# Four quantizer levels ahead of VectorE, and a transposed router product, in a fused weight-quantize and FFN kernel

## The chip, the cores and the metric

The kernel runs on one core of a Trainium2 chip. A core has five engines with a queue of instructions each: TensorE (PE; its weight loads are shown apart as PEld), VectorE (DVE), ScalarE (ACT), GpSimd (POOL) and SyncE (SP, which only issues DMAs here). The metric is the device time of one execution in microseconds; lower is better. Before the change it is 2672.33 us, the median of 3 runs (2671.02 to 2674.37).

## The reference

All is float32. Cut to what matters:

```python
# conditioner: a quantized linear layer with a low-rank part
lora_delta = lora_B @ lora_A * 0.5
cb = codebook / max(|codebook|)                    # 32 values
wg = (weight + lora_delta).reshape(O, I // 128, 128)
normalized = wg / exp(scale_log)
thresholds = (cb[:-1] + cb[1:]) * 0.5              # 31
idx = searchsorted(thresholds, normalized, side='left')
w = (cb[idx] - normalized) + normalized            # straight-through
w_eff = (w * scale).reshape(O, I) + lora_delta
c = x @ w_eff.T
# FFN: base product plus a mixture of 8 rank-16 experts
result = c @ W_base.T + b_base
ax, probs = c @ A_w.T, softmax(c @ router_w.T)
mixed = einsum(einsum(ax, cores), probs)
return x + result + (mixed @ B_w.T) * 2.0
```

x has 4096 rows of 2048, all weights are 2048 x 2048. The thresholds need not be sorted, so the kernel sorts them first and finds for each interval the value that the reference's search gives.

## The kernel before

The product x @ w_eff.T @ W_base.T is taken as x times one folded matrix. So there are two stages.

**Weight stage.** The quantized weight is made in 16 strips of 128 input columns (index i; a strip's tiles are w and a, 128 x 2048 each, in two halves f of 8 blocks). Each finished strip is multiplied with W_base into one strip of the folded matrix, and with the 24 columns of A_w and router_w (ra_sb) for the router.

A strip goes through these steps. In the strip before, its preparation: `delta` (TensorE, the low-rank part of w), `scaled` (ScalarE, half of a gets that part times a constant), `normalize` (GpSimd, w plus that, divided by the scale), `level_0` (ScalarE, Relu then Sign into sg, then Identity into a: the initial contents, the lowest value or the one after the first threshold) and `more_levels` (GpSimd, for levels 1 and 2: a compare-and-multiply into lv, line 526, and an addition to a, line 527). Then its own turn, `quantize`: for each level r from 3 to 30, `raise_to` lets ScalarE make a mask (line 537, Relu with a huge gain into float8, four buffers) and VectorE copies the level's value into a where the mask is set (line 538). Then `straight_through` (GpSimd, lines 557 to 559: minus w, plus w, times scale, half after half). Strip 0 has 29 full levels and two in halves, and its preparation is on VectorE.

The order of all other work is written out by hand. In strip i's turn, `behind(step, f, ...)` puts an operation behind the level of that step (step = r-3), in program order; each engine and each DMA queue then runs its own part of that order and waits for data or for a free buffer. In strip i's turn fall:
- at its start, the last quarter of products (3,1) of strip i-2, `route(i-2)`, `delta(i+1, 0)`;
- `products(i-1, ...)`: with blocks b of W_base, 0 and 1 kept on chip (wb), 2 and 3 streamed in quarters (wbp, three buffers, each `load_piece` on SP right after the quarter that it follows); blocks (2,0) first, then (3,1); `low_rank` ends each;
- `multiply_router(i-1)`: 16 matmuls with the strip as weights and 24 columns of ra_sb moving, and one for the low-rank part;
- `keep` (ScalarE copies a block from PSUM, a DMA writes it to wc_dram) and `keep_router` (copies 24 columns into rac);
- `load_w`, `load_la`, `load_route` (four tiles xs of xT) on SP. `route` is eight matmuls of 512 columns on a quarter of the array's columns each (line 642), adding the router's part for all tokens into acc. PSUM has three buffers m for products and router;
- from strip 5 to 15, `made`: one block of the folded matrix of four earlier strips (two blocks in strip 15) is fetched from wc_dram into up, transformed on GpSimd (`outer_w`, `inner_pair`, for a product that saves multiplications) and put into s_dram by SP. The fetch is at step 0, the rest at the steps of `step_of`.

After strip 15 come its own products, the last transforms (late_columns, and last_fetch with what follows it), with VectorE doing its straight-through in quarters.

**Main stage.** TensorE runs 196 products (line 909) of the transformed x (xA, xB, xC from xT, t on VectorE) with the tiles s of s_dram, two levels of a scheme with 7 products in place of 8; the other engines combine the results. Its code is not changed.

These few lines carry the preparation and the order before:

```python
for c in (1, 3):
    v.tensor_scalar(lv, half(i, f, "w"), base[:, c + 1 : c + 2], base[:, c : c + 1], ALU.is_gt, ALU.mult)
    v.tensor_tensor(a, a, lv, ALU.add)
```

Of the kernel before, what the change touches and what calls it, by code (L numbers as in the profile page):

```python
# [21 lines left out]
P = 128  # L22
# [4 lines left out]
MIX_SCALE = 32.0 / 16.0  # L27


def quantizer_tables(nc, work, const, psum, cb, index, beside):  # L30
# [109 lines left out]
    base = const.tile([P, 5], F32, name="base")  # L140
    v.tensor_tensor(base[:, 0:1], step[:, 0:1], cb[:, 0:1], ALU.subtract)
    next(beside, None)
    v.tensor_copy(base[:, 2:3], step[:, 0:1])
    next(beside, None)
    v.tensor_tensor(base[:, 1:2], step[:, 1:2], base[:, 2:3], ALU.subtract)
    next(beside, None)
    v.tensor_copy(base[:, 3:4], step[:, 1:2])
    next(beside, None)
    v.tensor_tensor(base[:, 3:4], step[:, 2:3], base[:, 3:4], ALU.subtract)
    next(beside, None)  # L150
    v.tensor_scalar(base[:, 2:5:2], neg_t[:, 1:3], -1.0 / GAIN, None, ALU.mult)
    next(beside, None)
    return neg_t, step, base
# [34 lines left out]
def adaln_ffn_kernel(  # L188
# [72 lines left out]
    nc.gpsimd.memset(rac, 0.0)  # L261
    cb = const.tile([P, K], F32, name="cb")
    ident = const.tile([P, P], F32, name="ident")
    ones = const.tile([P, 1], F32, name="ones")

# [7 lines left out]
    def constants():  # L273
        make_identity(nc, ident)
        nc.gpsimd.memset(cores_sb, 0.0)

        nc.gpsimd.tensor_copy(ones, ident[:, Q : Q + 1])
        for j in range(1, 4):
            nc.gpsimd.tensor_tensor(ones, ones, ident[:, RP * j + Q : RP * j + Q + 1], ALU.add)
        for j in range(4):  # L280
            nc.sync.dma_start(cores_sb[:, j, 0:Q], cores)
            for rows, what in ((slice(RP * j, RP * j + Q), bwT), (slice(RP * j + Q, RP * j + Q + 1), bias)):
                nc.sync.dma_start(
                    bw_sb[rows].rearrange("q (f n) p -> q f n p", n=2),
                    what.rearrange("q (f j n p) -> q j f n p", j=4, n=2, p=P)[:, j],
                )
# [80 lines left out]
    with ExitStack() as sa:  # L367
# [4 lines left out]
        xsp = sa.enter_context(tc.tile_pool(name="xsp", bufs=4))  # L372
# [61 lines left out]
        with tc.tile_pool(name="tables", bufs=1) as tables:  # L434
# [20 lines left out]
            neg_t, step, base = quantizer_tables(nc, tables, const, psum_t, cb, index, first_scales)  # L455
# [23 lines left out]
        ra_sb = cl.tile([P, NM, NRA], F32, name="ra_sb")  # L479
        nc.sync.dma_start(ra_sb, raT)  # L480
# [29 lines left out]
        def level_0(i, f, part):  # L510
            q, a = half(i, f, "w"), half(i, f, "a")
            if part == 0:
                strips[i]["sg"] = mpool0.tile([P, NM // 2, P], BF16, tag="sg", name=f"sg_{i}_{f}")
                nc.scalar.activation(strips[i]["sg"], q, AF.Relu, bias=neg_t[:, 0:1], scale=GAIN)  # L514
            sg = strips[i]["sg"]
            if part == 1:
                nc.scalar.activation(sg, sg, AF.Sign)
            if part == 2:
                nc.scalar.activation(a, sg, AF.Identity, bias=cb[:, 0:1], scale=base[:, 0:1])  # L519

        def more_levels(i, f):
            a = half(i, f, "a")
            lv = mpool0.tile([P, NM // 2, P], F32, tag="lv", name=f"lv_{i}_{f}")
            v = nc.gpsimd
            for c in (1, 3):
                v.tensor_scalar(lv, half(i, f, "w"), base[:, c + 1 : c + 2], base[:, c : c + 1], ALU.is_gt, ALU.mult)  # L526
                v.tensor_tensor(a, a, lv, ALU.add)  # L527

# [13 lines left out]
        def quantize(i, at):  # L542

            for r in range(3 if i else 2, T):
                raise_to(i, r, new_mask(i, r), 0, 1)
                for do in at.get(r - 3, []):
                    do()

# [14 lines left out]
        lora_r = cl.tile([R, NRA], F32, name="lora_r")  # L563
# [19 lines left out]
        def lora_router():  # L583
            ps = psum_m.tile([P, OQ], F32, tag="m", name="lc_r")
            for m in range(NM):
                nc.tensor.matmul(
                    ps[:R, :NRA], lora_B_sb[:, m, :], ra_sb[:, m, :], start=(m == 0), stop=(m == NM - 1)
                )
            nc.scalar.mul(lora_r, ps[:R, :NRA], LORA_SCALE)
# [24 lines left out]
        def multiply_router(i):  # L614
            ps = psum_m.tile([P, OQ], F32, tag="m", name=f"m_{i}_r")
            for m in range(NM):
                nc.tensor.matmul(
                    ps[:, :NRA], strips[i]["a"][:, m, :], ra_sb[:, m, :], start=(m == 0), stop=False
                )
            nc.tensor.matmul(ps[:, :NRA], strips[i]["la"][:R], lora_r, start=False, stop=True)  # L620
            strips[i]["r"] = ps

# [5 lines left out]
        def keep_router(i):  # L628
            nc.scalar.copy(rac[:, strip[i], 0:NRA], strips[i]["r"][:, :NRA])


        def load_route(i):
            strips[i]["x"] = []
            for n in range(4):
                x = xsp.tile([P, 2 * HT], F32, tag="xs", name=f"xs_{i}_{n}")
                nc.sync.dma_start(x, xT[ts(strip[i], P), ts(n, 2 * HT)])
                strips[i]["x"].append(x)

        def route(i):
            for n in range(8):  # L640
                j = n % 4
                nc.tensor.matmul(
                    acc[n // 4][RP * j : RP * j + RP],
                    rac[:, strip[i], :],
                    strips[i]["x"][n // 2][:, ts(n % 2, HT)],
# [77 lines left out]
        for i in range(NS):  # L723
# [5 lines left out]
            if i > 1:  # L729

                products(i - 2, (3, 1), NC - 1)
                route(i - 2)
                behind(5, keep, i - 2, 3)
                behind(6, keep, i - 2, 1)
            if i + 1 < NS:
                delta(i + 1, 0)
                if i > 0:
                    behind(3, load_w, i + 1)
                behind(7, scaled, i + 1, 0)
                behind(8, normalize, i + 1, 0)  # L740
                for f, (a, b, c) in enumerate(((10, 12, 14), (16, 18, 20))):
                    behind(a, level_0, i + 1, f, 0)
                    behind(b, level_0, i + 1, f, 1)
                    behind(c, level_0, i + 1, f, 2)
                    behind(c, more_levels, i + 1, f)
                behind(11, scaled, i + 1, 1)
                behind(11, normalize, i + 1, 1)
            if i > 0:


                behind(9, load_route, i - 1)
                for c in range(2):
                    behind(2 + 3 * c, products, i - 1, (2, 0), c)
                if i + 1 < NS:
                    behind(7, delta, i + 1, 1)
                for c in range(2, NC):
                    behind(2 + 3 * c, products, i - 1, (2, 0), c)
                behind(13, multiply_router, i - 1)
                behind(17, keep, i - 1, 2)
                behind(19, keep, i - 1, 0)  # L760
                for c in range(NC - 1):
                    behind((17, 20, 22)[c], products, i - 1, (3, 1), c)
                behind(22, keep_router, i - 1)
                if i + 2 < NS:
                    behind(20, load_la, i + 2)
            else:
                behind(4, nc.vector.reciprocal, rflat[:, NM:], flat[:, NM:])
# [3 lines left out]
                behind(26, lora_router)  # L771
            for n, (g, b) in enumerate(made.get(i, [])):
                step_of = (4, 9, 11, 12, 15, 26, 27) if len(made[i]) == 1 else (
                    (4, 6, 8, 9, 10, 12, 13) if n == 0 else (17, 19, 21, 22, 23, 25, 26)
# [30 lines left out]
        route(last - 1)  # L805
        keep(last - 1, 3)
        keep(last - 1, 1)
        load_route(last)
# [4 lines left out]
        for bs in ((2, 0), (3, 1)):  # L813
            for c in range(NC):
                products(last, bs, c)
            if bs[0] == 2:
                multiply_router(last)
            for b in bs:
                keep(last, b)
            if bs[0] == 2:  # L820
                keep_router(last)
                late_columns()
        route(last)
# [412 lines left out]
```

## Time and profile before

| | |
|---|---|
| median of 3 runs | 2672.33 us |
| the profiled execution, its own time | 2673.15 us |
| its span, first to last instruction | 2671.4 us |
| weight stage, first to last predicated copy | 19.2 to 1179.4 us |
| main stage's first product (line 909) | 1247.1 us |
| PE busy, share of the span | 2550.7 us, 95% |
| DVE busy | 1574.0 us, 59% |
| ACT busy | 1107.3 us, 41% |
| POOL busy | 1302.6 us, 49% |
| TensorE's mean granted clock | 0.973 |

In the profile's lines, an entry reads: line of the code, engine, operation, output <- inputs, shape, count. "Idle before" is how long the engine did nothing just ahead of it, and what ended that. A share over the whole span hides that there are two stages: VectorE is busy to the brim in the first and little used in the second. Stretches of the timeline tell more, and the start of line 557 marks the end of each strip.

### The profile page before, as it was taken

The numbers are of one execution on the slowest core, as the hardware profiler recorded it, in microseconds if no ns is written. First come the engines' busy times: TensorE is split into PE (matmuls) and PEld (weight loads), VectorE is DVE, ScalarE is ACT, GpSimd is POOL, SyncE is SP. The second block draws the span as 40 slices with busy tenths as digits, with TensorE's granted clock in tenths as the row PEclk, the third lists the DMA queues.
The fourth block names the chain that finished last, engine by engine and source line by source line (L and its number), as shares of the span: only waits on it lengthen the run. The fifth ranks groups of instructions, "written<-read, shape, count | busy, mean of one in ns | idle before, by whom it ended". The sixth has DMA issues, their size and how long they took to land.

```text
span 2671.4 us, 26221 instructions
## 1 busy us (share of the span) xinstructions
PE 2550.7 (95%) x10544; PEld 1758.3 (66%) x10544; DVE 1574.0 (59%) x996; ACT 1107.3 (41%) x740; POOL 1302.6 (49%) x755
## 2 busy tenths in 40 slices
PE   5599999999999999999999999999999999999999
PEld 2244444444444444446888888888888888888887
DVE  9999999999999999973433222242133322214221
ACT  7889988889888888940000000000000000000000
POOL 5566668889888888844413140042320323202224
PEclk9799999999999999999999999999999999999999
DMA  8254457767777766699844666545675455754554
GB/s 317 108 173 174 176 178 251 240 222 233 247 240 237 243 229 230 211 313 350 325 173 163 225 249 217 197 146 204 241 236 194 166 205 174 277 211 174 193 199 159
DMA packets 222041, 581.06 MB, mean 218 GB/s; under 512 B 18328, under 2 KB 119584, under 8 KB 176992
## 3 DMA queue, kind: packets, MB, share of 16 engines
q1 hardware_dynamic: 215360, 557.96, 60.7%
q0 software_dynamic: 4960, 14.95, 1.6%
q10 hardware_dynamic: 1600, 6.49, 0.6%
q8 instruction: 83, 1.36, 0.2%
q14 instruction: 38, 0.31, 0.0%
HBM read 477.62 MB, written 101.71 MB: 217 GB/s over the span
## 4 chain that ended last, share of the span: by engine, by line
PE 53%; DVE 25%; ACT 7%; POOL 6%; DMA 6%; issue 2%; SPq 0%; DVEq 0%; POOLq 0%; ACTq 0%
PE z L909 49%; DVE a L538 24%; ACT above L537 5%; DMA w<-in_weight 2%; PE m L606 2%; POOL a L558 1%; POOL a L557 1%; PE z L939 1%; DMA xA<-in_xT 1%; POOL w L505 1%; POOL a L559 1%; POOL w L430 1%; DMA wc_dram<-out 1%; ACT sg L514 1%; DMA s_dram<-late 1%
## 5 line engine op out<-in xcount | busy, mean ns | idle before, releaser
L538 DVE COPY_PREDICATED a<-above,step 128x2048 f32<-128x2048 uint8 (+1 forms) x453 | 1112.9, 2460 | 45.8 <-ACT above L537 1.5
L537 ACT ACTIVATE above<-w,neg_t 128x2048 fp8e5<-128x2048 f32 (+1 forms) x453 | 888.9, 1991 | 80.1 <-DVE a L538 67.1
L909 PE MATMUL z<-t,s 128*128 128x256 f32 x3584 | 793.0, 381 | 4.6 <-DVE u L991 4.6
L909 PEld LDWEIGHTS z<-t,s 128*128 128x128 f32 x3584 | 678.7, 190 | 108.5 <-issue 12.9
L606 PE MATMUL m<-wbp,a 128*128 128x512 f32 x1024 | 505.3, 640 | 74.8 <-POOL a L559 60.3
L606 PE MATMUL m<-wb,a 128*128 128x512 f32 x1024 | 460.7, 592 | 0.2
L606 PEld LDWEIGHTS m<-wbp,a 128*128 128x128 f32 x1024 | 205.3, 205 | 326.4 <-issue 243.0
L606 PEld LDWEIGHTS m<-wb,a 128*128 128x128 f32 x1024 | 193.7, 190 | 242.3 <-issue 237.2
L989 ACT COPY m<-z 128x1024 f32<-128x1024 f32 x28 | 28.4, 1013 | 763.3 <-PE z L909 763.3
L1000 POOL TENSOR_TENSOR c<-u,m 128x1024 f32<-128x1024 f32 x16 | 50.1, 3130 | 444.1 <-DVE u L997 422.8
L909 PE MATMUL z<-xA,s 128*128 128x256 f32 x1152 | 254.6, 379 | 0.0
L909 PEld LDWEIGHTS z<-xA,s 128*128 128x128 f32 x1152 | 218.8, 190 | 30.5 <-issue 0.8
L526 POOL TENSOR_SCALAR lv<-w,base 128x1024 f32<-128x1024 f32 x60 | 226.9, 3782 | 3.6
L1000 POOL TENSOR_TENSOR M<-u,m 128x1024 f32<-128x1024 f32 x8 | 24.8, 3103 | 330.2 <-DVE u L997 288.2
L909 PE MATMUL z<-xB,s 128*128 128x256 f32 x768 | 169.7, 379 | 0.0
L909 PE MATMUL z<-xC,s 128*128 128x256 f32 x768 | 169.7, 379 | 0.0
L991 DVE TENSOR_TENSOR u<-z,m 128x1024 f32<-128x1024 f32 x28 | 34.3, 1223 | 216.1 <-issue 172.6
L909 PEld LDWEIGHTS z<-xB,s 128*128 128x128 f32 x768 | 145.9, 190 | 19.8
L909 PEld LDWEIGHTS z<-xC,s 128*128 128x128 f32 x768 | 145.9, 190 | 19.8
L995 ACT COPY m<-z 128x1024 f32<-128x1024 f32 x28 | 28.3, 1011 | 308.5 <-PE z L909 308.5
L527 POOL TENSOR_TENSOR a<-a,lv 128x1024 f32<-128x1024 f32 x60 | 142.4, 2374 | 16.9 <-ACT a L519 12.3
L557 POOL TENSOR_TENSOR a<-a,w 128x1024 f32<-128x1024 f32 x30 | 71.3, 2378 | 145.0 <-DVE a L538 145.0
(208 smaller groups left out, 1922.8 us busy)
## 6 DMA issues: line engine op xcount, KB each, us to landing
s<-s_dram SPq DMA_DIRECT2D x196, 1024.0 KB, 4.8
wbp<-in_wbT SPq DMA_DIRECT2D x131, 1024.0 KB, 5.2
xs<-in_xT SPq DMA_DIRECT2D x64, 512.0 KB, 7.3
xA<-in_xT SPq DMA_DIRECT2D x24, 1024.0 KB, 9.1
s_dram<-z SPq DMA_DIRECT2D x84, 256.0 KB, 5.7
xB<-in_xT SPq DMA_DIRECT2D x16, 1024.0 KB, 10.8
outT<-M SPq DMA_DIRECT2D x16, 1024.0 KB, 10.6
w<-in_weight SPq DMA_DIRECT2D x15, 1024.0 KB, 7.7
```

The costliest lines, as they stand in the source:

```text
L430: v.tensor_tensor(w, w, r.unsqueeze(2).to_broadcast([P, NM // 2, P]), ALU.mult)
L526: v.tensor_scalar(lv, half(i, f, "w"), base[:, c + 1 : c + 2], base[:, c : c + 1], ALU.is_gt, ALU.mult)
L527: v.tensor_tensor(a, a, lv, ALU.add)
L537: nc.scalar.activation(above[:, c], q, AF.Relu, bias=neg_t[:, r : r + 1], scale=GAIN, saturate=False)
L538: nc.vector.copy_predicated(a, above[:, c].bitcast(U8), step[:, r : r + 1].to_broadcast([P, F // n]))
L557: v.tensor_tensor(a, a, w, ALU.subtract)
L606: nc.tensor.matmul(ps, strips[i]["a"][:, CM * c + m, :], t[:, m, :], start=c == 0 and m == 0, stop=False)
L909: nc.tensor.matmul(z[:, c, :], s[:, k, ts(c, P)], rhs[:, k, :], start=not more and k == 0 and c % PER == 0, stop=k == NK - 1 and c % PER = ...
L989: nc.scalar.copy(temp("m1", o), z["a"])
L991: nc.vector.tensor_tensor(temp("u2", o), z["b"], state["m1", o], ALU.add)
L995: nc.scalar.copy(temp("m5", o), z["c"])
L1000: lambda d: nc.gpsimd.tensor_tensor(d, state["u3", o], state["m5", o], ALU.add),
```

## The change

The constant NL = 4 is the number of levels that are in a before VectorE begins. Strips 1 to 15 now start `quantize` at r = 4, so step k is level k+4. Level 3 of half 0 is made by ScalarE (Relu, Sign, then a copy with a scale into a tile lx) and added to a by GpSimd (`last_level`). Level 3 of half 1 is made by GpSimd as levels 1 and 2 are, except for strips 6 to 15 (those prepared while GpSimd also has a transform; `half_step`), where VectorE still raises that half by a copy of 128 x 1024.

The router's product is transposed: the 32 columns of ra_sb (24 and zeros) are the weights, the strip moves, and the 16 matmuls go to four quarters of the array's columns in turn. `router_parts` (ScalarE) copies the four partial sums to raw, and `router_sum` (TensorE) adds and transposes them by a product with stack, four identities one above the other. `keep_router` now copies all 32 columns.

`route` and `load_route` are split into halves with two xs buffers in place of four; the second half is loaded at step 0 of the next strip and used at step 8. `load_w` comes at step 1 in two halves. Most steps of ScalarE's and GpSimd's work are new: the preparation of half 0 ends later, and `keep` of blocks 2 and 0 comes at steps 16 and 17.

```diff
+NL = 4
...
+    v.tensor_copy(rise[:, 1:NL], step[:, 0 : NL - 1])
+    v.tensor_tensor(rise[:, 0:1], step[:, 0:1], cb[:, 0:1], ALU.subtract)
+    v.tensor_tensor(rise[:, 1:NL], step[:, 1:NL], rise[:, 1:NL], ALU.subtract)
+    v.tensor_scalar(past, neg_t[:, 0:NL], -1.0 / GAIN, None, ALU.mult)
...
-    nc.gpsimd.memset(rac, 0.0)
...
+        nc.gpsimd.tensor_copy(stack, ident[:, 0:RP])
...
+            nc.gpsimd.tensor_tensor(stack, stack, ident[:, RP * j : RP * j + RP], ALU.add)
...
-        xsp = sa.enter_context(tc.tile_pool(name="xsp", bufs=4))
+        xsp = sa.enter_context(tc.tile_pool(name="xsp", bufs=2))
...
-        ra_sb = cl.tile([P, NM, NRA], F32, name="ra_sb")
-        nc.sync.dma_start(ra_sb, raT)
+        ra_sb = cl.tile([P, NM, RP], F32, name="ra_sb")
+        nc.vector.memset(ra_sb, 0.0)
+        nc.sync.dma_start(ra_sb[:, :, 0:NRA], raT)
...
-        def level_0(i, f, part):
+        def scalar_level(i, f, r, part):
...
-            if part == 2:
-                nc.scalar.activation(a, sg, AF.Identity, bias=cb[:, 0:1], scale=base[:, 0:1])
+            if part == 2 and r == 0:
+                nc.scalar.activation(a, sg, AF.Identity, bias=cb[:, 0:1], scale=rise[:, 0:1])
+            elif part == 2:
+                strips[i]["lx"] = mpool0.tile([P, NM // 2, P], F32, tag="lx", name=f"lx_{i}_{f}")
+                nc.scalar.activation(strips[i]["lx"], sg, AF.Copy, scale=rise[:, r : r + 1])
+
+        def half_step(i):
+            return i - 1 in made
...
-            for c in (1, 3):
-                v.tensor_scalar(lv, half(i, f, "w"), base[:, c + 1 : c + 2], base[:, c : c + 1], ALU.is_gt, ALU.mult)
+            for r in range(1, NL - 1 if f == 0 or half_step(i) else NL):
+                v.tensor_scalar(lv, half(i, f, "w"), past[:, r : r + 1], rise[:, r : r + 1], ALU.is_gt, ALU.mult)
                 v.tensor_tensor(a, a, lv, ALU.add)
+
+        def last_level(i, f):
+            a = half(i, f, "a")
+            nc.gpsimd.tensor_tensor(a, a, strips[i]["lx"], ALU.add)
...
-            for r in range(3 if i else 2, T):
+            if half_step(i):
+                raise_to(i, NL - 1, new_mask(i, NL - 1), 1, 2)
+            for r in range(NL if i else 2, T):
                 raise_to(i, r, new_mask(i, r), 0, 1)
...
         def multiply_router(i):
             ps = psum_m.tile([P, OQ], F32, tag="m", name=f"m_{i}_r")
             for m in range(NM):
+                j = m % 4
                 nc.tensor.matmul(
-                    ps[:, :NRA], strips[i]["a"][:, m, :], ra_sb[:, m, :], start=(m == 0), stop=False
+                    ps[RP * j : RP * j + RP, 0:P], ra_sb[:, m, :], strips[i]["a"][:, m, :],
+                    start=m < 4, stop=m >= NM - 4 and j > 0, tile_position=(0, RP * j),
+                    skip_group_check=True,
                 )
...
+        def router_parts(i):
+            nc.scalar.copy(raw, strips[i]["r"][:, 0:P])
+
+        def router_sum(i):
+            nc.tensor.matmul(strips[i]["r"][:, P : P + RP], raw, stack, start=True, stop=True)
...
                 products(i - 2, (3, 1), NC - 1)
-                route(i - 2)
-                behind(5, keep, i - 2, 3)
-                behind(6, keep, i - 2, 1)
+                route(i - 2, 0)
+                behind(0, load_route, i - 2, 1)
+                behind(2, keep, i - 2, 3)
+                behind(3, keep, i - 2, 1)
             if i + 1 < NS:
                 delta(i + 1, 0)
                 if i > 0:
-                    behind(3, load_w, i + 1)
-                behind(7, scaled, i + 1, 0)
-                behind(8, normalize, i + 1, 0)
...
+                    behind(1, load_w, i + 1, 2)
+                behind(4, scaled, i + 1, 0)
+                behind(4, normalize, i + 1, 0)
+                behind(10, scaled, i + 1, 1)
+                behind(10, normalize, i + 1, 1)
+                for r, f, parts in ((0, 0, (11, 12, 13)), (NL - 1, 0, (14, 15, 18)), (0, 1, (19, 20, 21))):
+                    for n, p in enumerate(parts):
+                        behind(p, scalar_level, i + 1, f, r, n)
+                behind(14, pool_levels, i + 1, 0)
+                behind(19, last_level, i + 1, 0)
+                behind(21, pool_levels, i + 1, 1)
             if i > 0:
-                behind(9, load_route, i - 1)
+                behind(9, load_route, i - 1, 0)
+                if i == NS - 1:
+                    behind(9, load_route, i - 1, 1)
...
+                if i > 1:
+                    behind(8, route, i - 2, 1)
...
-                behind(17, keep, i - 1, 2)
-                behind(19, keep, i - 1, 0)
+                behind(16, keep, i - 1, 2)
+                behind(17, keep, i - 1, 0)
...
-                behind(22, keep_router, i - 1)
+                behind(19, router_sum, i - 1)
+                behind(23, keep_router, i - 1)
+                behind(18, router_parts, i - 1)
...
-                step_of = (4, 9, 11, 12, 15, 26, 27) if len(made[i]) == 1 else (
-                    (4, 6, 8, 9, 10, 12, 13) if n == 0 else (17, 19, 21, 22, 23, 25, 26)
+                step_of = (3, 5, 10, 13, 17, 23, 25) if len(made[i]) == 1 else (
+                    (4, 6, 8, 9, 10, 12, 13) if n == 0 else (17, 19, 21, 22, 23, 24, 25)
                 )
...
             if bs[0] == 2:
                 multiply_router(last)
+                router_parts(last)
             for b in bs:
                 keep(last, b)
             if bs[0] == 2:
+                router_sum(last)
                 keep_router(last)
                 late_columns()
```

## The prediction

> **What bounds the kernel now.** I read the page's busy table, then the costliest groups, then the timelines of POOL, PE and ACT over one weight strip, then the windows of granted clock, and last the end of the weight stage. The page (its two costliest groups; count, then busy us and mean ns, then idle before):
> ```profile
> L538 DVE COPY_PREDICATED a<-above,step 128x2048 f32<-128x2048 uint8 (+1 forms) x453 | 1112.9, 2460 | 45.8 <-ACT above L537 1.5
> L537 ACT ACTIVATE above<-w,neg_t 128x2048 fp8e5<-128x2048 f32 (+1 forms) x453 | 888.9, 1991 | 80.1 <-DVE a L538 67.1
> ```
> VectorE's predicated copies fill 19.2 to 1179.4 us with 0.1 us between them: the weight stage is VectorE's. After it TensorE is the bound until the end. POOL's timeline (start, length, [idle before <- releaser]), end of one strip and a place in an early one:
> ```profile
> 809.39 2.38 POOL L527 TENSOR_TENSOR a<-a,lv 128x1024 f32<-128x1024 f32 x1
> 819.86 2.39 POOL L557 TENSOR_TENSOR a<-a,w 128x1024 f32<-128x1024 f32 x1 [8.09 <-DVE a L538]
> ...
> 217.44 3.78 POOL L526 TENSOR_SCALAR lv<-w,base 128x1024 f32<-128x1024 f32 x1
> 223.69 2.39 POOL L527 TENSOR_TENSOR a<-a,lv 128x1024 f32<-128x1024 f32 x1 [2.47 <-ACT a L519]
> ```
> L557 opens each strip's end on POOL; from one to the next is 71.93 us (72.28 after the first), 28 copies of 2.569. GpSimd has 8.09 us over, and its first compare of a half does not wait for ScalarE, only the addition does. PE in the same strip, and three restarts after idling:
> ```profile
> 785.05 4.11 PE L617 MATMUL m_r<-ra_sb,a 128*128 128x24 f32 x32
> 789.09 0.62 PE L620 MATMUL m_r<-lora_r,la 64*128 64x24 f32 x2
> 790.88 5.79 PE L606 MATMUL m<-wbp,a 128*128 128x512 f32 x8 [1.17 <-ACT out L625]
> ...
> 821.69 1.93 PE L642 MATMUL acc<-xs,rac 128*32 128x512 f32 x16
> 823.54 1.16 PE L411 MATMUL d<-la,lora_BT_sb 64*128 64x128 f32 x16
> 826.74 3.70 PE L606 MATMUL m<-wbp,a 128*128 128x512 f32 x8 [2.04 <-POOL a L559]
> ...
> 107.04 6.37 PE L606 MATMUL m<-wbp,a 128*128 128x512 f32 x8 [33.27 <-POOL a L559]
> 1114.51 3.70 PE L606 MATMUL m<-wbp,a 128*128 128x512 f32 x8 [3.33 <-POOL a L559]
> 1293.57 8.79 PE L909 MATMUL z<-t,s 128*128 128x256 f32 x32 [4.56 <-DVE u L991]
> ```
> TensorE idles only some 3 us per strip. It is a near second bound. Windows of those restarts and of one router product (columns: stretch, length, busy PE, PEld, DVE, ACT, POOL, granted clock, DMA):
> ```profile
> 107.00:112.40 5.40, 5.36 (x7) 2.27 (x8) 5.19 (x3) 4.27 (x4) 5.24 (x3) 0.50 0.00 0
> 1293.50:1296.80 3.30, 3.23 (x8) 2.58 (x9) 3.30 (x4) 0.00 (x0) 3.27 (x6) 0.50 0.89 326
> 860.00:872.00 12.00, 11.08 (x26) 5.79 (x26) 11.48 (x6) 12.00 (x10) 11.66 (x12) 0.72 0.62 186
> ```
> The clock is half after the router product, and after idling 4.56 or 33 us; after 3.33 us eight matmuls took the usual 3.70.
>
> **The change, part by part.** I count t from a strip's L557, and K is the time at which ScalarE starts keep of block 2.
>
> *VectorE.* Fifteen full copies go (15 x 2.569 = 38.5); ten halves come, for strips 6 to 15, at 1.38 (shortest form 1.29 plus the 0.09 between): 13.8. Net 24.7 us is the most the stage can give. Floors: 27 x 2.569 = 69.4 for strips 1 to 5, 70.74 from 6 on.
>
> *ScalarE.* A mask takes 1.9 back to back (six in 11.48), Relu 1.04, Sign 0.94, Identity 1.13, keep 0.46, scaled 0.90 (start to start). A made strip holds 27.5 masks 52.2, nine half-operations 9.3, two scaled 1.8, four keeps 1.8, router copies 0.2: 65.4 of 70.74. It fits, but order decides. Four mask buffers hold the mask of step k until VectorE has freed k-4, so step 10 starts at 18.1 (19.4 with the half copy). Adding what follows up to step 16, ScalarE reaches keep 2 at t=37.4 (38.7).
>
> *The added wait.* Keep 2 now stands where TensorE has barely finished block (2,0). Before, that took from 826.74 to 857.04, which is 30.3; half a route is put inside (0.96); it starts at 6.9. So K cannot be before 38.2, plus c, what a restart at half clock costs. Behind keep 2 in ScalarE's queue stand six masks, the copy lx and the last Relu, Sign, Identity; VectorE and GpSimd wait for these. For c: the router product shrinks, so TensorE idles about 70.7-62.2-1.4-c, some 5 us, per strip. The 3.33 us row gives c=0; the 4.56 us row 8.79-7.07=1.7; the 33 us row 6.37-3.60=2.8. Between the last two, nearest the 4.56 row, I take 2.1: K=40.3.
> The Trainium skill, "TensorE: Matmul & The Clock Gate", Part 1, lets an idle window of about 3.4 us halve the clock, and a busy window of 3.4 us restore it, which would speak against a change that empties TensorE. The 4.56 and 33 us rows agree. By that rule 3.4 to 6.8 us run at half after a restart, an estimate of c=2.6 on average; the sum below would be about 2 us smaller.
>
> *GpSimd.* From K to the last Identity of half 1 is 14.9 (two keeps 0.92, five masks 9.5, lx 1.13, router copy 0.15, Relu 1.04, Sign 0.94, Identity 1.23). Without transform work (strips 1 to 4 while preparing 2 to 5) half 1 then gets three levels; the first compare is already done, so addition, two compares, two additions follow: 2.48+3.87+2.48+3.87+2.37=15.1. The strip lasts K+30.1 = 70.4 (71.92 before): 1.5 each for strips 2 to 4, together 4.6. Strip 1 has no route inside but restarts after 30 us: keep follows the old end of the product at 39.9, giving 69.95 against 72.28: 2.3. In strip 0 the last Identity ends at about 82 and GpSimd at 97.1, before VectorE's 100.2: nothing. From strip 5 on: 13.55 straight-through, 4.95 outer, 8.5 normalize, 10.5 inner, 12.5+2.4+12.5 levels = 65 of 70.7; done about t=68, hidden.
>
> *Does VectorE starve behind keep 2?* At K=40.3 the mask of step 22 is ready at 57.1 and wanted at 57.9 in a half-copy strip, all earlier ones with more room. Strip 5 has no half copy and stalls 0.55: 69.95, gain 2.0. Strips 6 to 14 run at their floor: 9 x 1.19 = 10.7.
>
> *TensorE's router.* Sixteen matmuls of 128 columns, four column groups. By L642 (eight of 512 columns in 1.93) 1.0; by L411 (128 columns, two abreast, 1.16 for eight) 2.3; at worst the old 4.7. I take 1.4 with lora_r and the sum. Off the path: it ends before POOL frees the next strip unless router and c exceed 8.5. router_sum waits for raw (K+6.1=46.4); TensorE gets there at about 48.
>
> *SP.* load_route of half 1 goes ahead of the fetch and waits for route on TensorE (t about 1); fetch, queued behind it, issues by 4 and lands by 9 to 13 (7.0 median, 8.4 longest, and 1 MB ahead), wanted at 13.55: hidden; later, it delays normalize, Relu and K. load_w at step 1 waits till 11.7 as before; behind it two writes of wc_dram and one wbp piece lose some 1 us, used 15 us later. Its two halves cost one issue of 0.35 and let normalize start sooner. With two xs buffers each load waits for one route half, 15 us or more ahead of use.
>
> *Start.* The tables lose two tiny VectorE operations and gain a memset of ra_sb (POOL's same-sized one took 0.53): between -0.3 and +0.5, I take 0. stack is made while GpSimd idles 13.41; ra_sb in 96-byte rows is first read at 70.7, having landed 20.8 after its issue at 15.8.
>
> *End of the stage.* The chain of waits leaves VectorE at 1153.7 for the second transform set of strip 15:
> ```profile
> 1155.52 5.17 DMA wc_dram<-out
> 1185.01 11.74 DMA wc_dram<-out
> 1196.77 23.27 DMA xA<-in_xT
> ```
> From 1190 to 1290 the DMA share is about 1.0. In strip 15 SP passes the third wbp piece at t=24.3; the route half and c push that to about 27.3, and the puts, the second fetch and xs, xA with it: +3.0. The other path, through the last products, has VectorE -1.2 but keep behind router and raw +1.8: +0.6. I take +1.5. TensorE's own gain there (some 3 us) only lengthens the 4.56 wait; its restart may cost 0.5 more than 1.7.
>
> **Sum**, against the profiled execution of 2673.15 (span 2671.4; 0.8 over the median 2672.33): 2.3+4.6+2.0+10.7 = 19.6 until strip 15, less 1.5 and 0.5: 17.6. 2673.15-17.6-0.8 = 2654.7, say 2655.
>
> **Rivals.**
> 1. *ScalarE's margin is eaten.* VectorE starves from K=41.1. For: 0.8 us of margin; c of 2.8 nearly uses it. Against: ScalarE is full ahead again by step 4. With K at 42.1, 1 us in some eleven strips: 2665.
> 2. *Slower: the fetch lands late.* Queued behind load_route, it holds outer_w, normalize and, through Relu, every later mask. Until a landing at 17.2 K hides it; beyond, each us costs nine strips 1 us. The 17.6 gain is gone at 19.2; at 19.8 it is 2678, slower. For: xs loads took up to 8.3. Against: some 4 us between the expected landing and the wish, and DMA engines that are a third idle in these strips.
> 3. *The router does not shrink.* Should the column groups run one by one with the clock halved, TensorE's strip is 62.2+6.7+3.4=72.3: 2674, no gain. Against: L642's eight matmuls ran four abreast.
> 4. *All hidden.* c=0 and a rigid end: 2648.
>
> **How the numbers follow.** Forecast 0.62 (2648 to 2662); rival 1 0.18, a third of it within the bound; rival 2 0.10; rival 3 0.04; rival 4 0.06. What a measurement can tell is about 0.2%, 5.3 us. Faster 0.62+0.12+0.06=0.80, same 0.10, slower 0.10. The range 2647 to 2668 leaves out rivals 2 and 3 and the tail of rival 1.
>
> **What would show it.** Right: 405 full and ten half copies after strip 0, L557 70.7 apart from strip 6 and about 70.4 in strips 2 to 4; ScalarE waiting some 2 us for TensorE at keep 2; half clock at strip starts and no longer after the router; its 32 matmuls in 1 to 2.3 us. Wrong: VectorE waiting for masks every strip, POOL's outer waiting for up, L557 still 72 apart, or the wait at 1293 grown past 13 us.

## The result, and the profile after

The changed kernel takes 2672.31 us, the median of 12 runs (2666.77 to 2676.03); the kernel before took 2672.72 in 12 runs beside them (2670.11 to 2677.38). The ratio is 0.9996, 95% interval 0.9987 to 1.0004. A later series gave 0.9982 (0.9973 to 0.9991). So the change is worth between nothing and 0.3%; 0.66% was forecast. The forecast, 2655 in a range from 2647 to 2668, missed: no gain of that size is there. The profiled execution (2666.77, span 2665.0) happens to be the shortest of the twelve; a second profile, below, had a span of 2670.0.

The two costliest groups of VectorE and ScalarE after the change, from the page:

```profile
L550 DVE COPY_PREDICATED a<-above,step 128x2048 f32<-128x2048 uint8 (+1 forms) x448 | 1090.2, 2436 | 61.1 <-ACT above L549 19.3
L549 ACT ACTIVATE above<-w,neg_t 128x2048 fp8e5<-128x2048 f32 (+1 forms) x448 | 872.4, 1976 | 55.1 <-DVE a L550 44.5
```

VectorE has 22.7 us less to do (1112.9 before), nearly the 24.7 expected, but its idle time has risen from 45.8 to 61.1, and 19.3 us of that ends with a mask from ScalarE (1.5 before). TensorE around the start of strip 10's turn (start, length, [idle before <- releaser]; compare the 3.70 us restart after 2.04 of idle before):

```profile
744.50 1.16 PE L410 MATMUL d<-la,lora_BT_sb 64*128 64x128 f32 x16
750.40 6.17 PE L621 MATMUL m<-wbp,a 128*128 128x512 f32 x8 [4.74 <-POOL a L574]
756.40 0.39 PE L625 MATMUL m<-ident 128*128 128x128 f32 x2
756.63 3.60 PE L621 MATMUL m<-wb,a 128*128 128x512 f32 x8
760.06 3.60 PE L621 MATMUL m<-wbp,a 128*128 128x512 f32 x8
763.50 3.60 PE L621 MATMUL m<-wb,a 128*128 128x512 f32 x8
767.02 1.16 PE L410 MATMUL d<-la,lora_BT_sb 64*128 64x128 f32 x16
...
784.10 1.08 PE L634 MATMUL m_r<-a,ra_sb 128*32 128x128 f32 x32
785.11 0.40 PE L639 MATMUL m_r<-la,lora_r 64*32 64x128 f32 x2
```

The router's product has shrunk from 4.11 to 1.08 us, even more than forecast, TensorE now idles 4.74 us before a strip, and the first eight products cost 6.17 us in place of 3.70. The second half of delta follows two quarters later and ends at 768.2. ScalarE in the same stretch:

```profile
762.75 2.00 ACT L549 ACTIVATE above<-w,neg_t 128x2048 fp8e5<-128x2048 f32 x1 [0.57 <-DVE a L550]
768.23 1.02 ACT L502 ACTIVATE a<-d 128x1024 f32<-128x1024 f32 x1 [3.48 <-PE d L410]
...
785.62 0.56 ACT L654 COPY out<-m 128x512 f32<-128x512 f32 x1
```

There it is: `scaled` of the second half (line 502) waits 3.48 us for that delta. It waited for nothing before. At the copy of block 2 (line 654, 785.62), where the forecast looked for a wait, there is none: ScalarE comes late by then. ScalarE reaches that copy 42.1 us after the strip's start (743.53) in place of the forecast 38.7; the 3.48 us make the difference. Some 11 us after it VectorE begins to run out of masks:

```profile
796.53 2.46 DVE L550 COPY_PREDICATED a<-above,step 128x2048 f32<-128x2048 uint8 x1 [0.22 <-ACT above L549]
799.37 2.47 DVE L550 COPY_PREDICATED a<-above,step 128x2048 f32<-128x2048 uint8 x1 [0.38 <-ACT above L549]
802.40 5.04 DVE L550 COPY_PREDICATED a<-above,step 128x2048 f32<-128x2048 uint8 x2 [0.56 <-ACT above L549]
```

The sums from 100 to 1180 us, by the view of waits (total us, times, longest), show the wait of line 502 once in each of strips 1 to 14, and VectorE's 49 waits for masks beside it:

```profile
PE m L621 <- POOL a L574: 101.0, 15, 34.7
POOL a L572 <- DVE a L550: 62.3, 11, 6.2
ACT a L502 <- PE d L410: 49.8, 14, 5.5
...
DVE a L550 <- ACT above L549: 19.3, 49, 0.6
```

And the windows of granted clock (stretch, length, busy PE, PEld, DVE, ACT, POOL, clock, DMA share, GB/s): half speed has moved from behind the router product to the strips' starts.

```profile
748.40:755.20 6.80, 4.80 (x6) 2.19 (x7) 6.49 (x4) 6.73 (x5) 6.60 (x3) 0.51 0.62 190
784.00:788.00 4.00, 3.27 (x40) 1.81 (x39) 3.90 (x2) 4.00 (x4) 3.92 (x2) 1.00 1.06 359
860.00:872.00 12.00, 12.00 (x31) 5.37 (x30) 11.44 (x6) 12.00 (x10) 11.46 (x11) 1.00 0.59 196
```

At the end of the stage a second new wait stands. ScalarE writes block (15,2) 7.4 us after it has copied it, the next copy waits, and TensorE behind it (two views):

```profile
1206.74 0.59 ACT L654 COPY out<-m 128x512 f32<-128x512 f32 x1
1214.72 0.34 ACTq L655 DMA_DIRECT2D wc_dram<-out  x1
1215.10 0.59 ACT L654 COPY out<-m 128x512 f32<-128x512 f32 x1 [7.77 <-DMA xA<-in_xT]
...
1215.74 5.40 PE L621 MATMUL m<-wb,a 128*128 128x512 f32 x8 [4.43 <-ACT out L654]
1288.53 7.17 PE L954 MATMUL z<-t,s 128*128 128x256 f32 x32 [1.71 <-DVE u L1036]
```

The write waits for a DMA that it has nothing to do with, the load of xA. In the built program each of these DMAs signals on one of eight semaphores, taken in turn, and is issued only when the DMA before it on the same one has landed; here that is the second half of xA, which takes 23 us.

Where the time went, as differences to the profile before (us; a strip is from one first straight-through to the next; the second profile and the last column are of the runs a_again and e8_early_old_router below):

| | forecast | changed | changed, 2nd profile | old router, early delta |
|---|---|---|---|---|
| first straight-through (100.20 before) | 0 | +0.54 | +0.58 | +0.13 |
| strip 1 | -2.3 | +0.35 | -0.88 | -2.22 |
| strips 2 to 4 | -4.6 | -3.07 | -1.04 | -7.30 |
| strip 5 | -2.0 | -0.96 | -0.91 | -2.47 |
| strips 6 to 14 | -10.7 | -2.93 | -2.88 | -9.13 |
| strip 15 to its last copy | | -0.78 | -0.79 | -1.09 |
| from there to the end of the main stage's first wait for VectorE (1293.57 before) | +2.0 with the line above | +1.79 | +3.71 | +3.85 |
| the rest | 0 | -1.36 | +0.8 | +1.22 |
| span | -17.6 | -6.4 | -1.4 | -17.0 |

### The profile page after: what moved, and what is told of

Same layout as the page of the kernel before. It is cut to its first block, busy times and chain, and to the rows that moved or that the text cites. A ratio compares the mean times of both kernels' runs of the same rounds, so it can differ in the third digit from the quotient of the medians.

```text
span 2665.0 us, 26423 instructions
## 1 busy us (share of the span) xinstructions
PE 2503.9 (94%) x10576; PEld 1704.1 (64%) x10576; DVE 1549.0 (58%) x990; ACT 1130.1 (42%) x796; POOL 1367.2 (51%) x783
## 3 DMA queue, kind: packets, MB, share of 16 engines
q1 hardware_dynamic: 219296, 557.96, 61.1%
q8 instruction: 83, 1.36, 0.2%
## 4 chain that ended last, share of the span: by engine, by line
PE 62%; ACT 17%; DVE 8%; POOL 7%; DMA 3%; issue 2%; SPq 0%; DVEq 0%; ACTq 0%; POOLq 0%
PE z L954 49%; ACT above L549 11%; PE m L621 10%; DVE a L550 7%; ACT sg L516 2%; ACT sg L519 2%; POOL a L572 1%; POOL a L573 1%; PE z L984 1%; ACT a L521 1%; POOL lv L534 1%; POOL a L574 1%; POOL a L535 1%; DMA xA<-in_xT 1%; DMA wc_dram<-out 1%
## 5 line engine op out<-in xcount | busy, mean ns | idle before, releaser
L550 DVE COPY_PREDICATED a<-above,step 128x2048 f32<-128x2048 uint8 (+1 forms) x448 | 1090.2, 2436 | 61.1 <-ACT above L549 19.3
L549 ACT ACTIVATE above<-w,neg_t 128x2048 fp8e5<-128x2048 f32 (+1 forms) x448 | 872.4, 1976 | 55.1 <-DVE a L550 44.5
L534 POOL TENSOR_SCALAR lv<-w,past,rise 128x1024 f32<-128x1024 f32 x65 | 245.9, 3783 | 3.7
L535 POOL TENSOR_TENSOR a<-a,lv 128x1024 f32<-128x1024 f32 x65 | 154.3, 2374 | 27.1 <-ACT a L521 21.0
L1042 DVE TENSOR_TENSOR u<-z,u 128x1024 f32<-128x1024 f32 x28 | 34.3, 1223 | 119.8 <-PE z L954 81.3
```

Of the source, the lines that this page charges most:

```text
L534: v.tensor_scalar(lv, half(i, f, "w"), past[:, r : r + 1], rise[:, r : r + 1], ALU.is_gt, ALU.mult)
L549: nc.scalar.activation(above[:, c], q, AF.Relu, bias=neg_t[:, r : r + 1], scale=GAIN, saturate=False)
L550: nc.vector.copy_predicated(a, above[:, c].bitcast(U8), step[:, r : r + 1].to_broadcast([P, F // n]))
L1042: nc.vector.tensor_tensor(temp("u3", o), z["d"], state["u2", o], ALU.add)
```

## The experiments

Theory 1: the second half of delta, behind two quarters of products that start with a cold TensorE (one whose granted clock is half), makes `scaled` late, and this starves VectorE. Theory 2: ScalarE has too much to do, and any wait taken away returns as another. Theory 3: the write that waits for xA gives part of the gain back.

### Delta earlier

```diff
-                    behind(7, delta, i + 1, 1)
+                    behind(4, delta, i + 1, 1)
```

> One edit to the changed kernel: the second half of delta goes from step 7 to step 4, so TensorE makes it after one quarter of products instead of two; nothing else moves. Theory 1 (ScalarE's second scaled waits for TensorE's second delta, which stands behind two quarters done by a cold TensorE, and this lateness starves VectorE): the wait of scaled on d falls from 49.8 us in the weight stage to under 15, VectorE's idle time of about 0.93 us per strip from strip 6 on goes, the strips come at 70.7 to 70.9 us, the last predicated copy ends at about 1160 (1172.5 in the changed kernel, 1179.4 before), and the time is 2658 to 2664. Theory 2 (ScalarE has simply too much to do, 65.4 of 70.7 us and its own overheads, so that a wait taken away comes back as another): the wait on d falls too, but the strips stay at 71.5 and the time at 2670 to 2674.

Measured: 2660.94 us, ratio 0.9954 (0.9942 to 0.9967). The last predicated copy ends at 1163.45 (1172.52 in the changed kernel), strips 6 to 14 take 70.9 or 71.3. Its waits:

```profile
ACT above L549 <- DVE a L550: 48.2, 88, 0.9
ACT out L654 <- PE m L609: 41.8, 20, 6.4
```

The wait of line 502 on delta is gone from the list. TensorE's restarts are as cold as before (5.13 to 6.72 us). Theory 2 falls: ScalarE does the same work, and from strip 6 on VectorE waits for a mask once, for 0.46 us. What comes next is the wait that the forecast named, ScalarE at the copy of block 2, 1.2 to 3.9 us in each strip. Two expectations missed: the last copy is 3 us later than 1160, with strips 3 and 4 at 71.0 and 71.3, and four of the strips 6 to 14 take 71.3 in place of at most 70.9. One thing besides the order changed: the wait for xA at the end of the stage is gone too (the write of block (15,2) now follows another DMA on its semaphore). The runs under "The end of the stage" show that this alone gains nothing that the times can tell.

### A warm TensorE, the order unchanged

The repeated calls issue the first half's matmuls again, with the same data into the same place in PSUM.

```diff
                 delta(i + 1, 0)
+                for _ in range(4 if i else 0):
+                    delta_again(i + 1)
```

> One addition to the changed kernel: TensorE repeats the first half of delta four times, with the same data into the same place, at the start of strips 1 to 14, about 1.16 us each, so that it does not idle 4.7 to 5.6 us there; the second half of delta stays behind two quarters. It separates the two parts of theory 1, the cold restart and the place in the order. If the cold restart is what makes scaled late: the clock stays full at the strips' starts, the first eight products take 3.6 instead of 6.2 us, scaled's wait falls from 3.5 to about 1 us per strip, and VectorE's stalls shrink to under 0.2 us; the strips come at about 70.8 to 71.0 and the time is 2660 to 2666. If the place in the order is enough by itself: the wait falls by 2.5 us but the strips stay above 71.4, 2668 to 2673. By theory 2: no change, 2670 to 2674.

Measured: 2661.75 us, ratio 0.9956 (0.9942 to 0.9969), last copy at 1166.05. More work for TensorE makes the kernel 0.3% faster than the changed one. It did not keep TensorE warm everywhere, and this makes the run tell more. Strips 10 and 11 (lines 421 and 631 are delta_again and the products here, 512 is scaled):

```profile
745.41 3.70 PE L631 MATMUL m<-wbp,a 128*128 128x512 f32 x8 [1.20 <-POOL a L584]
760.78 1.02 ACT L512 ACTIVATE a<-d 128x1024 f32<-128x1024 f32 x1 [0.92 <-PE d L410]
...
816.41 6.74 PE L631 MATMUL m<-wbp,a 128*128 128x512 f32 x8 [2.96 <-POOL a L584]
834.81 1.02 ACT L512 ACTIVATE a<-d 128x1024 f32<-128x1024 f32 x1 [3.68 <-PE d L410]
```

Strip 10 took 71.02 us, strip 11 72.24. Same code, same order; only the restart differs. In numbers:

| strips of this run | restart | wait of scaled | strip |
|---|---|---|---|
| 6, 8, 10, 12, 14 | 3.70 | 0.67 to 0.92 | 71.0 to 71.4 |
| 13 | 5.09 | 2.12 | 71.29 |
| 7, 9, 11 | 6.58 to 6.74 | 3.61 to 3.90 | 71.85 to 72.24 |
| 2 to 5 | 3.70 | 2.12 to 2.20 | 69.55 to 70.10 |

Strips 6, 8, 11 and 13 have a stall of 0.46 us that comes from elsewhere (see "Open"). Without it a wait of 2 us costs nothing, one of 3.6 to 3.7 us some 0.8 us per strip, one of 3.9 some 1.2. The write of block (15,2) waits for xA here as in the changed kernel (6.9 us behind its copy), so the gain does not come from there.

### The changed kernel again

> The changed kernel itself once more, for a second profile and for times on the chip of the other three. If the distance between its profile (2666.8 us) and its median (2672.3) lies in the weight stage, because the moment at which TensorE's clock drops and recovers decides how long scaled waits, this profile shows other strip lengths, a last predicated copy 2 to 6 us away from 1172.5, and a time that is off by the same amount. If it lies in the main stage, the last copy is again within 1 us of 1172.5 and the first wait of the main stage again ends near 1288.5, and only what follows is longer.

Measured: 2671.61 us, ratio 0.9982 (0.9973 to 0.9991); the profile's span is 2670.0. Its last copy ends at 1173.44, 0.9 later than in the first profile, and the first wait of the main stage ends at 1291.37, 2.8 later; the remaining 2.2 us lie behind it. So neither place alone makes the distance. One strip shows theory 1 within one and the same kernel. Strip 2 in the first profile, then in the second:

```profile
180.23 3.70 PE L621 MATMUL m<-wbp,a 128*128 128x512 f32 x8 [3.45 <-POOL a L574]
```

```profile
179.04 5.62 PE L621 MATMUL m<-wbp,a 128*128 128x512 f32 x8 [5.16 <-POOL a L574]
```

After 3.45 us of idle the restart was warm, scaled waited 2.16 and the strip took 69.64; after 5.16 it was cold, scaled waited 4.11 and the strip took 71.50.

### The old router product

The router's product, `lora_r`, `ra_sb` and `keep_router` are as before the change; `router_parts` and `router_sum` are gone:

```diff
...
-                    ps[RP * j : RP * j + RP, 0:P], ra_sb[:, m, :], strips[i]["a"][:, m, :],
-                    start=m < 4, stop=m >= NM - 4 and j > 0, tile_position=(0, RP * j),
-                    skip_group_check=True,
+                    ps[:, :NRA], strips[i]["a"][:, m, :], ra_sb[:, m, :], start=(m == 0), stop=False
...
-                behind(19, router_sum, i - 1)
-                behind(18, router_parts, i - 1)
```

> The router's part of the change alone is undone in the changed kernel: its product is again 16 matmuls with the strip as weights and 24 columns moving, without raw and router_sum; the level, the new order and the halves of route stay. TensorE then has some 3 us more work per strip and less to idle. Theory 1 (cold restarts make the second delta late): the idle time at the strips' starts falls under 3.4 us, the first eight products take 3.7 us again instead of 6.2, scaled's wait falls from 3.5 to under 1.5 us, VectorE's stalls nearly go, the last copy ends 4 to 9 us before 1172.5, and the time is 2660 to 2668, so that the cheaper router product costs time within this change. Rival (the place in the order alone counts, or TensorE with the old router becomes the bound): strips of 71.5 or more, 2670 to 2680.

Measured: 2662.51 us, ratio 0.9945 (0.9930 to 0.9960), last copy at 1161.28. Undoing the cheaper router makes the changed kernel 9 us faster (2671.6 beside it). Eight of the strips 6 to 14 take 70.9 to 71.0; strip 9, with a restart of 6.72 and a wait of 3.98, takes 72.06. One expectation missed: the restart is not always 3.70. It is 5.40 in strips 6, 7 and 12 after 3.73, 3.09 and 1.64 us of idle and 5.17 in strip 11 after 2.92, with waits of 2.4 to 2.7 that VectorE does not feel; strip 4 restarts cold too (5.40 after 3.34), waits 3.87 and takes 71.13.

### Both causes taken away

Early delta and repeated delta, the two edits shown above together:

> The early second delta and the repeated first delta together. With the early delta alone the second wait of my forecast appeared (ScalarE at the copy of block 2 waits 2.1 us for TensorE, 20 times), and strips 3 and 4 still took 71.0 and 71.3 us; with the repetition alone strips 3 to 5 took 69.6 to 70.1, but strips 7, 9 and 11 still 71.9 to 72.2. If both waits come from a cold restart and from the order, each on its own: strips 2 to 5 at 69.6 to 70.1, 6 to 14 at 70.9 to 71.3, the last copy at 1157 to 1161, and the time 2652 to 2659. If something else holds the strips from 6 on: last copy 1163 or later, 2659 to 2664.

Measured: 2657.31 us (2656.52 to 2658.41), ratio 0.9929 (0.9917 to 0.9941), last copy at 1160.90. Strips 2 to 5 take 69.4 to 70.1, strips 6 to 14 70.9 to 71.3. The early delta with the old router, and no repeated work:

> The old router product and the early second delta together, with no repeated work. The old router alone gave strips of 70.9 us in eight of the nine from strip 6 on, with waits of scaled of up to 4.0 us where a restart was cold (strips 4 and 9: 71.1 and 72.1). With the early delta these waits have no place left: strips 1 to 5 at 69.5 to 70.2, 6 to 14 at 70.9, last copy at 1158 to 1161, time 2655 to 2661, level with the early delta and the repeated first delta together (2657.3). If TensorE, fuller by some 3 us per strip, becomes the bound once VectorE runs free, strips from 6 on come at 71.2 or more and the time is 2662 or more.

Measured: 2658.89 us (2655.80 to 2660.31), ratio 0.9937 (0.9924 to 0.9951), last copy at 1157.28. Every strip from 2 to 5 takes 69.4 to 69.7, every one from 6 to 14 70.87 to 70.99, and VectorE's whole wait for masks over the stage is

```profile
ACT out L640 <- PE m L609: 43.1, 17, 8.8
```
```profile
L550 DVE COPY_PREDICATED a<-above,step 128x2048 f32<-128x2048 uint8 x416 | 1017.3, 2449 | 42.3 <-ACT above L549 1.0
```

1.0 us (the second fence, groups of VectorE from 100 to 1160 us: busy, mean ns | idle before <- releaser), while ScalarE waits 43.1 us for TensorE at the copies of blocks (the first, from the view of waits) and has the margin for it: ten of the 17 waits, of 1.1 to 4.4 us, are at block 3 in the first microseconds of a strip, six of 0.2 to 3.1 at block 2, and the longest at the end of the stage. These two kernels beat both the changed kernel and the one before; their intervals overlap, so which is the better is open.

### The end of the stage

Strip 15's router copy behind the copies of its blocks, and block 0 ahead of block 2:

```diff
             if bs[0] == 2:
                 multiply_router(last)
-                router_parts(last)
-            for b in bs:
+            for b in reversed(bs):
                 keep(last, b)
             if bs[0] == 2:
+                router_parts(last)
                 router_sum(last)
```

> One edit to the end of the weight stage of the changed kernel: behind strip 15's router product ScalarE first copies and writes blocks 0 and 2 and only then copies raw; by this order the two writes no longer take the places in the turn of DMAs that the second half of xA holds. The strips before are untouched (71.5 us each, last copy at about 1172.5). Theory 3 (the write of block (15,2) waits for xA, holds the next copy and through it TensorE, and gives part of the stage's gain back): TensorE's 4.43 us in front of the first quarter of blocks 3 and 1 goes, the first main product starts at about 1239 instead of 1244.6, and the wait that follows in the main stage ends 3 to 5 us earlier, at 1284 to 1286; the time is 2667 to 2670. Its rival (the tail is held by the transforms and by memory traffic): the first main product also comes earlier, but the wait after it grows by as much, still ends at about 1288.5, and the time is 2671 to 2674.

Measured: 2669.76 us, ratio 0.9982 (0.9973 to 0.9991). TensorE's 4.43 us are gone, the write follows its copy at once, and the first main product comes at 1241.63 (1244.58 in the changed kernel), but the first wait of the main stage grows from 1.71 to 3.81 and ends at 1287.14, only 1.4 earlier. The same edit on top of the early delta:

> The edits of the two kernels before together. If theories 1 and 3 both hold and the two places are independent: the last predicated copy ends at about 1160, the wait at the start of the main stage ends 14 to 17 us before that of the kernel before (1293.6), and the time is 2653 to 2660. If only theory 1 holds: 2658 to 2664. If only theory 3 holds: 2667 to 2670. If neither holds: 2671 to 2674.

Measured: 2664.95 us, ratio 0.9964 (0.9951 to 0.9978), no better than the early delta alone. The wait for xA is back, now at the second write: the early delta shifts by one place which semaphore xA's second half gets, and TensorE waits 7.85 us for raw, which stands behind that write in ScalarE's queue. One more run moves no work at all, only the turn (n is 2 for one piece of strip 15 and 1 for all others):

```diff
-                q.dma_start(t, wbT[b][:, ts(c, CM), :])
+                for h in range(n):
+                    m = ts(h, CM // n)
+                    q.dma_start(t[:, m], wbT[b][:, ts(c, CM), :][:, m])
```

> One edit to the changed kernel that moves no work: the one of strip 15's last weight pieces that ScalarE loads third is fetched by two DMAs of half the size. All DMAs behind it come one place later in the turn of eight, so the write of block (15,2) follows another DMA than the second half of xA. If the turn of eight is what made that write wait 7.4 us: it is issued right after its copy, the next copy follows at once, TensorE's wait of 4.43 us and its 5.40 us restart go, and the first main product comes at about 1239. If the write waits for its queue or for traffic: it is still issued near 1214.7. In both cases the strips are as in the changed kernel, and by the run with the other order of copies the time gains at most some 3 us: 2667 to 2672.

Measured: 2669.61 us, ratio 0.9981 (0.9971 to 0.9990). ScalarE at that place:

```profile
1208.67 0.59 ACT L656 COPY out<-m 128x512 f32<-128x512 f32 x1
1209.29 0.34 ACTq L657 DMA_DIRECT2D wc_dram<-out  x1
1209.67 0.58 ACT L656 COPY out<-m 128x512 f32<-128x512 f32 x1 [0.41 <-ACT out L656]
```

The write goes out right behind its copy: the turn of eight was the cause of the 7.4 us. TensorE's 4.43 us are gone and the first main product comes at 1240.12, but it then waits 5.91 us ahead of the second group of main products, and the first wait for VectorE ends at 1293.61 (the profile is of the slowest of its ten executions, 2674.74). The ratio is that of the changed kernel on the same chip (0.9982), as it is with the other order of copies. So theory 3 holds as a mechanism and falls as a price: the wait is real, and what is saved there comes back as waits at the start of the main stage. What sets their end is not shown.

## Why the prediction was wrong

**The step that failed** is the one on ScalarE: "Adding what follows up to step 16, ScalarE reaches keep 2 at t=37.4 (38.7)". It added durations and no waits, though `scaled` of half 1 at step 10 needs TensorE's second delta. The forecast held all the numbers for it. Step 10 starts at 19.4 in a strip with a half copy, and one mask later, at 21.3, scaled is due; measured, ScalarE was free at 21.2 (768.23 less 3.48, from 743.53). TensorE starts at 6.9, needs 14.15 for two quarters (754.82 to 768.97 before) and 1.1 for delta: 22.2 with a warm clock, 24.3 with the c of 2.1 that the forecast itself took, 24.7 measured. So keep 2 came not at 38.7 but at 42.1, which is 38.7 + 3.48 but for 0.1. A wait of 0.9 was there to be read even without a cold restart (0.92 measured with the warm TensorE), and of 3 with it. Before the change scaled stood at step 11 and began at 774.87 in that strip, 4.7 us after its delta (768.97 + 1.16), so nothing in that profile shows the wait.

**c** was 2.1 and measured 6.17 - 3.70 = 2.5 in strip 10 (2.3 to 2.6 in strips 6 to 14): the right mechanism and nearly the right size, applied to block (2,0) only and not to the delta in its middle.

**Keep 2.** Its added wait, K = 38.2 + c, did not show in the changed kernel, as ScalarE came later than that. With the early delta it does, and its consequence comes out as worked: strips 2 to 4 were to last K + 30.1 = 68.3 + c; their restarts of 5.40, 6.31 and 6.65 make that 70.0, 70.9 and 71.25, and they took 70.10, 70.99 and 71.32. The path is the one worked out: in these strips GpSimd goes from the last addition straight to the straight-through, without idling. In the changed kernel the same sum holds with the later ScalarE: in strips 2 to 4 it reaches keep 2 at 39.6, 41.5 and 41.6, and they take 69.64, 71.50 and 71.57, 30.0 more each.

**VectorE and the floors.** 405 full copies and ten halves followed strip 0, and the floors were right: 70.87 to 70.99 against 70.74 and 69.4 against 69.4 where nothing else held the strip. The 10.7 us of strips 6 to 14 became 2.9; with the old router and the early delta they are 9.1. That the gain in the profiled span of that kernel is 17.0 us, near the 17.6 forecast, is luck: it leaves out the new router product, it is put together differently (22.1 until the last copy, less 5.1 after it), and its median lies 2.4 above the profiled execution.

**Rivals.** The outcome is of rival 1's kind, VectorE behind a late ScalarE, but at another place, and in nearly every strip from the start: it priced 1 us in some eleven strips for a K of 42.1. That relation was right: with K at 41.7 to 42.1, strips 6 to 14 took 71.3 to 71.95, on average 0.9 above the floor. What was wrong is where the lateness was looked for: at keep 2 only. Rival 2 did not occur: GpSimd's first transform of strip 10 starts at 757.07, directly behind the straight-through that ends at 757.1, without waiting for the fetch. Rival 3's mechanism is refuted by the 1.08 us, rival 4's c of 0 by the 6.17. GpSimd had its room at the strip's end (5.89 us idle at 815.22) as forecast.

**End of the stage.** +2.0 was forecast for strip 15 and what follows; 1.0 and 2.9 were measured in the two profiles of the changed kernel. The reason given was that SP issues xA 3.0 later in the strip. Counted from the start of strip 15 it does so at 88.3 us before the change and at 88.9 and 91.4 in these two profiles, which goes with the 1.0 and 2.9. But in the kernel with the old router and the early delta it is on time (88.3), and strip 15 and what follows still cost 2.8, so it is not the only reason. The wait of a write for xA was not foreseen and costs next to nothing. What costs the 3.8 us in the kernel with the old router and the early delta stays open.

**Open** besides: a stall of VectorE of 0.46 us at the same step of strips 4, 6, 8, 11, 13 and 15 in every profile with the new router (71.3 against 70.9 where nothing else holds the strip) and in none with the old one, whether or not masks are late, and the 2 to 3 us by which the main stage differs between runs of like kernels.

## What to carry to other kernels

Where an engine's work is re-ordered, list for each moved instruction which other engine's result it needs and when that result is ready after the change, not before it; a sum of durations along one queue is only a lower bound. Where an edit empties an engine whose clock is throttled, the time it saves can come back as a cold restart, and whatever stands early behind that restart in its order, and has a reader with little slack, belongs ahead of the long work. Removing work from an engine that is off the bound can cost time on the one that is: here, with the rest of the change in place, the cheaper router product cost 9 us.

## What the runs showed of the hardware

How long TensorE may idle before a restart is cold was not one number here. Restarts (eight products of 512 columns at a strip's start) were warm (3.70 us) after up to 3.45 us of idle and always cold after 3.51 us or more. In between the same idle time gave both: 1.64 us gave 5.40 in strip 12 of the run with the old router and 3.70 in strip 8 of the kernel before, and 2.96 us gave 6.74 in one run and 3.70 in another. A cold restart cost 1.4 to 3.1 us. The Trainium skill, "TensorE: Matmul & The Clock Gate", Part 1, says that the gate watches a free-running window of about 3.4 us; that restarts after the same idle time differ from strip to strip agrees with it.

The idle time just ahead is not all that counts. TensorE around that restart of strip 12, then windows of the same run, then windows of the kernel before inside a router product (24 columns moving, from 856.97 to 861.30):

```profile
882.10 1.16 PE L411 MATMUL d<-la,lora_BT_sb 64*128 64x128 f32 x16
884.90 5.40 PE L621 MATMUL m<-wbp,a 128*128 128x512 f32 x8 [1.64 <-POOL a L574]
```
```profile
884.00:885.00 1.00, 0.10 (x1) 0.10 (x1) 0.90 (x2) 1.00 (x2) 1.00 (x2) 1.00 0.90 279
886.00:887.00 1.00, 1.00 (x2) 0.34 (x1) 0.92 (x1) 1.00 (x3) 1.00 (x1) 0.50 0.97 347
```
```profile
858.00:859.00 1.00, 1.00 (x11) 1.00 (x11) 0.90 (x2) 1.00 (x1) 1.00 (x1) 1.00 1.01 328
860.00:861.00 1.00, 1.00 (x7) 1.00 (x6) 0.90 (x2) 1.00 (x2) 0.90 (x2) 0.50 1.15 344
```

In strip 12 the clock fell only after the restart had begun, with the narrow products of delta ahead of the idle time. In the kernel before it fell with TensorE busy all the time, on narrow products. So where the same page and section says that the clock falls after at least one idle window, such a window need not be one without matmuls. What the gate counts as idle no run here shows.

Keeping TensorE busy with repeated products until the strip starts raised its mean granted clock from 0.975 to 0.986. And a DMA can be held for 7.4 us by one that is unrelated to it, through the semaphore that they share in turn; splitting one load elsewhere in two moved that wait away.
